# A two-layer graph network kernel: the first layer's row terms are spread by two DMAs instead of TensorE transposes, and the stages around them are reordered

## The chip, the cores and the metric

The kernel runs on one core of a Trainium2 chip. The metric is device time in microseconds (us); lower is better. The core has five engines that matter here: PE (TensorE, matrix products; PEld is its weight load), DVE (VectorE), ACT (ScalarE), POOL (GpSimd) and SP (SyncE, which here only issues DMAs). Each engine runs its own instructions strictly in their written order and waits where one of them needs a result that isn't there yet.

## The reference

Input `x` is 64 batches of 256 rows of 256 values; `adj` is one 256 x 256 adjacency mask for all batches. Two layers follow, each an attention over the graph and then a feed-forward part:

```python
x = x + _L0_gnn_ref(_layernorm(x), adj, L0_gnn_W, L0_gnn_a)   # 4 heads of 64
x = x + _L0_ffn_ref(_layernorm(x), L0_ffn_weight, L0_ffn_bias) # dense 256 -> 256
x = x + _L1_gnn_ref(_layernorm(x), adj, L1_gnn_W, L1_gnn_a)   # 1 head of 256
x = x + _L1_ffn_ref(_layernorm(x), L1_ffn_...)                 # 8 experts, top 2
```

In the first attention, `q = h @ W` is split into 4 heads; each row i has a term `e_src[i]` and each row j a term `e_dst[j]` per head; the score is `leaky_relu(e_src[i] + e_dst[j], 0.2)`, masked by `adj`, softmaxed over j, and multiplied with `q`. An elu follows.

## The kernel before

Everything is float32. A batch lies as 128 partitions x 2 halves (`NT` = 2) of rows. The softmax is computed without a sum in the exponent: since exp(max(a, b)) = max(exp a, exp b), the kernel takes exponentials of the row terms alone and forms each score as max(column value of i, scalar of j) times the mask. The scalar of j is a per-partition operand; the value of i has to stand in every partition along the free axis. That second form is the "row terms" of the change.

**What one batch does**, in `batch_layers`, a generator in which each `yield` ends a stage. `turned` (L114) turns blocks of x on DVE; `norm_stats` (L362) gives the norm's mean and variance on DVE and ends with two small POOL operations (L382, L383); `projected` (L429) multiplies with the weights on PE (L436) and takes three exponentials per head on ACT (L444); `scaled` (L449, L452) scales the values on DVE. `scores` (L500) then does, for two heads at a time, four PE transposes of one broadcast column each (L506), which put the row term of every i into all partitions of a PSUM bank, and four DVE operations (L513) that form the scores `z`. `attended` (L519) multiplies `z` with `q` on PE (L527) and inverts the sums (L534). DVE scales by them (L570), or ACT in the first 16 batches (`EARLY`, L565); ACT takes an exponential (L576) and DVE ends the elu and adds x (L579, L580, L583). The feed-forward part is a transpose on PE with a copy on ACT (`transposed`, L420, L426), a product (L591) and a DVE sum (L598) that gives `x2`. `norm_squares` (L392) squares on ACT (L401) and ends with two POOL operations (L411, L414). The second attention is `projected1` (L471, L478 to L484), `scores1` (L490, L495), `attended` and a relu on ACT (L614), with a DVE sum (L620) and squares again. Then `by` (L628, L631), the normalised rows and the base of the output on ACT (L640, L645), the store of the base by SP (L656), and the router's product (L670).

**The experts.** `route` decides for each chunk of batches which rows go where; POOL sends the rows to DRAM by indirect DMAs (L970). `expert_pair` loads 256 rows of one expert (SP, L804, L815) and its weights (L830), turns them on DVE (L116), multiplies twice on PE (L862 with Gelu on ACT L868; L877), DVE adds the bias (L887), ACT scales (L855), and POOL adds the rows into the output by indirect DMAs (L898). Two pairs run per batch once rows are there.

**What sets the order.** It is written out by a loop over steps, three to a batch (`TICKS`, phases 0, 1 and 2). In each step every active batch and job advances by one stage, in the order of the rank it yielded: a small rank is early in the step. A negative rank continues within the same step. So a batch's stages are spread over some 19 steps, and stages of about seven batches alternate in one period of three steps. A new batch begins in phase 2 at rank 25. All engines see their instructions in this order.

**Buffers.** `z` (6 buffers of 2 KB per partition), `xin` (6, loaded 3 batches ahead), the 8 PSUM banks that all products share. DMAs of SP and ACT share eight semaphores in turn; each waits for the one that last used its semaphore.

Of the kernel before, what the change touches and what calls it, by code (L numbers as in the profile page):

```python
# [9 lines left out]
F32 = mybir.dt.float32  # L10
I32 = mybir.dt.int32
AF = mybir.ActivationFunctionType
# [3 lines left out]
P = 128  # L16
# [11 lines left out]
def kernel(  # L28
# [17 lines left out]
    nc = tc.nc  # L46
# [47 lines left out]
    def load_batch(b):  # L94
        t = io.tile([P, NT, D], F32, tag="xin", name=f"xin_{b}", bufs=6)
        nc.sync.dma_start(
            out=t, in_=x_rows[b * N : (b + 1) * N, :].rearrange("(t p) d -> p t d", p=P)
        )
        return t
# [10 lines left out]
        return t  # L110

    S = 32

    def turned(dst, blocks):  # L114

# [371 lines left out]
    def scores1(ex, me):  # L487
        pd = bank("pd", [N])
        for t in range(NT):
            nc.tensor.transpose(  # L490
                pd[:, t * P : (t + 1) * P], ex[:, t, 1:2].to_broadcast([P, P]), ident
            )
        z = work.tile([P, NT, N], F32, tag="z", name="z", bufs=6)
        for j in range(NT):
            nc.vector.scalar_tensor_tensor(  # L495
                z[:, j, :], pd, ex[:, j, 2:3], me[:, j, :], op0=ALU.max, op1=ALU.mult
            )
        return z

    def scores(q, heads, hs, mask, probs):  # L500

        d = D // heads
        pd = bank("pd", [len(hs), N])
        for i, h in enumerate(hs):
            for t in range(NT):
                nc.tensor.transpose(  # L506
                    pd[:, i, t * P : (t + 1) * P],
                    q[:, t, h, d + 1 : d + 2].to_broadcast([P, P]), ident,
                )
        for i, h in enumerate(hs):  # L510
            z = work.tile([P, NT, N], F32, tag="z", name="z", bufs=6)
            for j in range(NT):
                nc.vector.scalar_tensor_tensor(  # L513
                    z[:, j, :], pd[:, i, :], q[:, j, h, d + 2 : d + 3], mask[:, j, :],
                    op0=ALU.max, op1=ALU.mult,
                )
            probs.append(z)

    def attended(q, heads, probs):  # L519

        d = D // heads
        pvs = []
        for t in range(NT):
            pv = bank("pv", [heads, d + 1])
            for h, z in enumerate(probs):
                for j in range(NT):
                    nc.tensor.matmul(  # L527
                        pv[:, h, :], z[:, j, t * P : (t + 1) * P], q[:, j, h, : d + 1],
                        start=(j == 0), stop=(j == NT - 1),
                    )  # L530
            pvs.append(pv)
        rinv = small.tile([P, NT, heads], F32, tag=f"rinv{heads}", name="rinv")
        for t, pv in enumerate(pvs):
            nc.vector.reciprocal(rinv[:, t, :, None], pv[:, :, d : d + 1])  # L534
        return pvs, rinv

    def batch_layers(b, c0, xng, lg):

        xb = xblk.pop(b)
        if b + BLOCKS_AHEAD < B:  # L540
            xblk[b + BLOCKS_AHEAD] = load_blocks(b + BLOCKS_AHEAD)
        xT = turned(work.tile([P, KT, N], F32, tag="xT", name="xT", bufs=4), xb)
# [12 lines left out]
        yield 10  # L555
        scores(q, H, range(2, 4), masks[0], probs)
        yield 50
        pvs, rinv = attended(q, H, probs)
# [38 lines left out]
        for t in range(NT):  # L597
            nc.vector.scalar_tensor_tensor(  # L598
                x2[:, t, :], pf[:, t, :], rstd[:, t : t + 1], x1b[:, t, :],
                op0=ALU.mult, op1=ALU.add, accum_out=sums[:, t : t + 1],  # L600
            )
# [8 lines left out]
        pvs, rinv = attended(q[:, :, None, :], 1, [z])  # L610
# [351 lines left out]
    def begin(job, rank):  # L962
        active.append([rank, len(order), job])
        order.append(job)
# [255 lines left out]
```

## Time and profile before

| | us |
|---|---|
| runs | 1582.44, 1584.82, 1584.85 (median 1584.82) |
| the profiled execution's own time | 1584.91 |
| its span, first to last instruction | 1583.0 |

All times of single operations below come from that one execution. The page's slices show how the busy share (in tenths) and the granted PE clock run over the 40 equal slices of the span:

```profile
PE   6999898899999999999999999999899998879996
DVE  6777777888888878888887878888788879555543
ACT  2676666576776777777777677667568898654332
PEclk9999999999999999999999999999999999889999
DMA  5721323456566657566666656675666766687853
```

Three stages can be told apart. Up to some 300 us few or no expert pairs are there; then the work of a batch and of two pairs repeats with a period of 21.33 us; after some 1300 us the batches are through the first layer and the remaining pairs and the dense last batches are worked off. The groups of the first layer's attention, costliest first (line, engine, operation, output<-input, shapes, count, then busy us, mean ns of one, idle time before and who ended it):

```profile
L527 PE MATMUL pv<-q,z 128*128 128x65 f32 (+1 forms) x2560 | 372.7, 300 | 5.9 <-issue 4.5
...
L436 PE MATMUL pq<-wx,xT 128*128 128x268 f32 x512 | 134.7, 408 | 3.2 <-DVE xT L116 2.6
```

The busy time of a PE group counts what isn't overlapped by the matmul before, so it is less than count times mean.

### The profile page before, as it was taken

Reading aid. Unit: us, or ns where it says so; the run is one execution under the profiler, and the core shown is the slowest. Engines: PE = TensorE matmul, PEld = TensorE weight load, DVE = VectorE, ACT = ScalarE, POOL = GpSimd, SP = SyncE. Lnnn points to the kernel's source line nnn. Section 1 sums busy time; section 2 is a strip of 40 time slices with the busy share of each in tenths; the row PEclk is TensorE's granted clock in tenths of the full one; section 3 lists DMA queues with packets and bytes.
Section 4 is the critical chain, followed back from the end, with each engine's and each line's share of the span. In section 5 each row is a group of like instructions: output and inputs, shape, how many; then the busy total and the mean of one; then the engine's idle time right before and its main releaser. Section 6 shows DMA issues by size and latency. Waiting matters only on the chain. (4 is left out here: it accounts for less than half of the span.)

```text
span 1583.0 us, 30896 instructions
## 1 busy us (share of the span) xinstructions
PE 1492.3 (94%) x8570; PEld 1316.6 (83%) x8570; DVE 1205.1 (76%) x4281; ACT 1044.4 (66%) x2515; POOL 862.5 (54%) x867
## 2 busy tenths in 40 slices
PE   6999898899999999999999999999899998879996
PEld 5888787788888888888888888888789887658885
DVE  6777777888888878888887878888788879555543
ACT  2676666576776777777777677667568898654332
POOL 2222536255756656565747575665665676743444
PEclk9999999999999999999999999999999999889999
DMA  5721323456566657566666656675666766687853
GB/s 147 217 55 48 94 69 88 114 125 138 140 137 149 146 115 156 128 153 131 159 132 130 140 141 137 149 147 110 155 135 147 145 139 120 140 193 169 158 100 50
DMA packets 361514, 207.61 MB, mean 131 GB/s; under 512 B 261496, under 2 KB 331648, under 8 KB 361344
## 3 DMA queue, kind: packets, MB, share of 16 engines
q1 hardware_dynamic: 311488, 138.31, 35.8%
q0 software_dynamic: 48864, 66.33, 23.0%
q8 instruction: 71, 1.16, 0.3%
q10 hardware_dynamic: 992, 0.99, 0.2%
q14 instruction: 99, 0.81, 0.2%
HBM read 117.43 MB, written 88.09 MB: 130 GB/s over the span
## 5 line engine op out<-in xcount | busy, mean ns | idle before, releaser
L898 POOL DMA_INDIRECT out_dram<-y,xt x258 | 412.0, 1597 | 176.8 <-issue 58.5
L527 PE MATMUL pv<-q,z 128*128 128x65 f32 (+1 forms) x2560 | 372.7, 300 | 5.9 <-issue 4.5
L527 PEld LDWEIGHTS pv<-q,z 128*128 128x128 f32 x2560 | 333.1, 194 | 19.6 <-issue 4.7
L877 PE MATMUL py<-w2s,hT 128*128 (+1 forms) x1224 | 284.8, 384 | 5.8 <-ACT hT L868 5.2
L970 POOL DMA_INDIRECT xs<-xng,pos x244 | 254.5, 1043 | 65.4 <-issue 60.7
L877 PEld LDWEIGHTS py<-w2s,hT 128*128 128x128 f32 x1224 | 230.4, 192 | 39.0 <-ACT hT L868 8.3
L862 PE MATMUL ph<-sT,we 128*128 128x256 f32 x1032 | 238.7, 381 | 3.3 <-DVE ohs L1099 2.9
L426 ACT COPY xT<-pt 128x512 f32<-128x512 f32 x192 | 113.3, 590 | 191.2 <-PE pt L420 142.5
L862 PEld LDWEIGHTS ph<-sT,we 128*128 128x128 f32 x1032 | 192.3, 191 | 28.4 <-DVE ohs L1099 3.3
L513 DVE SCALAR_TENSOR_TENSOR z<-pd,q,mask 128x256 f32<-128x256 f32 x512 | 211.2, 476 | 0.8 <-PE pd L506 0.8
L855 ACT ACTIVATE y<-y,w 128x256 f32<-128x256 f32 x258 | 112.5, 501 | 96.6 <-DVE y L887 87.6
L868 ACT ACTIVATE hT<-ph,we 128x256 f32<-128x256 f32 x306 | 123.4, 472 | 62.7 <-PE ph L862 40.9
L401 ACT ACTIVATE off<-x,sums 128x256 f32<-128x256 f32 x256 | 131.1, 512 | 40.3 <-DVE x L598 17.9
L471 PE MATMUL pq<-wx,xT 128*128 128x259 f32 x512 | 129.3, 394 | 19.3 <-ACT xT L426 11.7
L411 POOL TENSOR_SCALAR rstd<-sq 128x4 f32<-128x4 f32 (+1 forms) x66 | 12.8, 193 | 246.4 <-ACT off L401 246.1
L887 DVE TENSOR_TENSOR y<-py,b2s 128x512 f32<-128x512 f32 x129 | 86.9, 688 | 68.4 <-PE py L877 50.2
L436 PE MATMUL pq<-wx,xT 128*128 128x268 f32 x512 | 134.7, 408 | 3.2 <-DVE xT L116 2.6
L471 PEld LDWEIGHTS pq<-wx,xT 128*128 128x128 f32 x512 | 92.1, 190 | 45.8 <-ACT xT L426 19.9
L591 PE MATMUL pf<-wfT,xT 128*128 128x256 f32 x512 | 124.0, 386 | 0.1
L382 POOL TENSOR_SCALAR rstd<-mv 128x4 f32<-128x4 f32 (+1 forms) x66 | 15.4, 233 | 197.7 <-DVE mv L375 163.3
L436 PEld LDWEIGHTS pq<-wx,xT 128*128 128x128 f32 x512 | 99.4, 198 | 22.6 <-DVE xT L116 1.9
L591 PEld LDWEIGHTS pf<-wfT,xT 128*128 128x128 f32 x512 | 94.6, 195 | 10.9 <-DVE y L887 0.3
(165 smaller groups left out, 2552.5 us busy)
## 6 DMA issues: line engine op xcount, KB each, us to landing
we<-wpack SPq DMA_DIRECT2D x145, 288.0 KB
xr<-xs SPq DMA_DIRECT2D x516, 64.0 KB
xblk<-in_x_dram SPq DMA_DIRECT2D x256, 64.0 KB
xin<-in_x_dram SPq DMA_DIRECT2D x64, 256.0 KB
out_dram<-base SPq DMA_DIRECT2D x61, 256.0 KB
out_dram<-y,xt POOLq DMA_INDIRECT x258
xs<-xng,pos POOLq DMA_INDIRECT x244
xs<-fill SPq DMA_DIRECT2D x9, 260.0 KB
```

Of the source, the lines that this page charges most:

```text
L401: nc.scalar.activation(off, src[:, t, :], AF.Square, bias=sums[:, t : t + 1], scale=-float(D), accum_out=sq[:, at + t : at + t + 1],)
L426: nc.scalar.copy(dst, pt)
L436: nc.tensor.matmul(pq.rearrange("p h c -> p (h c)"), xT[:, k, t * P : (t + 1) * P], wx[:, k, :], start=(k == 0), stop=(k == KT - 1),)
L471: nc.tensor.matmul(pq, xT[:, k, t * P : (t + 1) * P], wx1[:, k, :], start=(k == 0), stop=(k == KT - 1),)
L513: nc.vector.scalar_tensor_tensor(z[:, j, :], pd[:, i, :], q[:, j, h, d + 2 : d + 3], mask[:, j, :], op0=ALU.max, op1=ALU.mult,)
L527: nc.tensor.matmul(pv[:, h, :], z[:, j, t * P : (t + 1) * P], q[:, j, h, : d + 1], start=(j == 0), stop=(j == NT - 1),)
L591: nc.tensor.matmul(pf[:, t, :], xT[:, k, t * P : (t + 1) * P], wfT[:, k, :], start=(k == 0), stop=(k == KT - 1),)
L862: nc.tensor.matmul(ph[:, f, :], we[:, k * D + f * P : k * D + (f + 1) * P], xT[:, k, :], start=(k == 0), stop=(k == KT - 1),)
L868: nc.scalar.activation(hT[:, f, :], ph[:, f, :], AF.Gelu, bias=we[:, C_B1 + f : C_B1 + f + 1])
L877: nc.tensor.matmul(py[:, t, :], hT[:, f, t * P : (t + 1) * P], w2s[:, e, f * D : (f + 1) * D].rearrange("p e c -> p (e c)"), start=(f == 0 ...
L898: d = nc.gpsimd.indirect_dma_start(out=out_rows, out_offset=bass.IndirectOffsetOnAxis(ap=xt[:, t, 0:1].bitcast(I32), axis=0), in_=y[:, t, ...
L970: d = nc.gpsimd.indirect_dma_start(out=xs_d[: E * CAP * PAIR, :], out_offset=bass.IndirectOffsetOnAxis(ap=at, axis=0), in_=xe, in_offset=None,
```

## The change

Four things change in `batch_layers` and its helpers.

1. **Row terms.** `scores` no longer transposes on PE. After `scaled`, `send_terms` turns the columns around the exponentials of `q` in 32 x 32 blocks on DVE into a small tile `ut`, so that a row term of 32 rows lies in one partition. An ACT-issued DMA writes 32 such runs (4 KB) to a DRAM tile of this batch. In the next step `spread_terms` issues, also from ACT, a DMA that reads the 4 KB into all 128 partitions, straight into the second half of the score tile `z4` (two buffers of 8 KB per partition). The score operations on DVE read it there, the last of them in place. `scores1` has its own tile `z1`.
2. **Stages of the first layer.** A batch (but the first) begins in phase 0, at rank 40, with the norm of x alone and then passes one step; the turn of x stays where it was. The projection moves from phase 1 to phase 0 (rank 60, its scaling and the first DMA at 65); the spreading takes phase 1 (rank 54); the scores stay in phases 2 and 0. The number of steps from the turn of x on is the same.
3. **The second layer's order.** Both `norm_squares` move to the start of the following step (ranks 7 and 6). The transposes of `x2` follow the first squares in the same step at rank 36, and so stand ahead of the second attention's product (rank 40). `by` is at rank 45, and the normalised rows and the base follow in the same step at rank 50.
4. **Early batches.** L565 on ACT is gone: DVE scales in every batch.

```diff
+    G = P // S
...
-        z = work.tile([P, NT, N], F32, tag="z", name="z", bufs=6)
+        z = work.tile([P, NT, N], F32, tag="z1", name="z1", bufs=1)
...
+    def send_terms(q, b):
+        ut = small.tile([P, S], F32, tag="ut", name="ut", bufs=1)
+        nc.vector.transpose(
+            ut.rearrange("p (t h w) -> p t h w", t=NT, h=H), q[:, :, :, HD - 1 : HD + 3]
+        )
+        ud = tc.dram_tile([S, S], F32, name=f"terms_{b}")
+        ud = ud.rearrange("c r -> (c r)").rearrange("(c p) -> c p", p=P)
+        return ut, ud
+
+    def spread_terms(ud):
+        z = work.tile([P, NT, NT, H, P], F32, tag="z4", name="z4", bufs=2)
+        nc.scalar.dma_start(
+            out=z[:, NT - 1].rearrange("p t h i -> p (t h i)"),
+            in_=rows_to_all(ud, S * S),
+        )
         return z
 
-    def scores(q, heads, hs, mask, probs):
-        d = D // heads
-        pd = bank("pd", [len(hs), N])
-        for i, h in enumerate(hs):
-            for t in range(NT):
-                nc.tensor.transpose(
-                    pd[:, i, t * P : (t + 1) * P],
-                    q[:, t, h, d + 1 : d + 2].to_broadcast([P, P]), ident,
-                )
-        for i, h in enumerate(hs):
-            z = work.tile([P, NT, N], F32, tag="z", name="z", bufs=6)
+    def scores(q, z, hs):
+        for h in hs:
             for j in range(NT):
                 nc.vector.scalar_tensor_tensor(
-                    z[:, j, :], pd[:, i, :], q[:, j, h, d + 2 : d + 3], mask[:, j, :],
+                    z[:, j, :, h, :], z[:, NT - 1, :, h, :], q[:, j, h, HD + 2 : HD + 3],
+                    masks[0][:, j, :].rearrange("p (t i) -> p t i", t=NT),
                     op0=ALU.max, op1=ALU.mult,
                 )
...
+        def first_norm():
+            x0 = xin.pop(b)
+            if b + AHEAD < B:
+                xin[b + AHEAD] = load_batch(b + AHEAD)
+            return x0, norm_stats(x0)[1]
+
+        if b:
+            x0, rstd = first_norm()
+            yield 99
+            yield 25
         xb = xblk.pop(b)
...
         xT = turned(work.tile([P, KT, N], F32, tag="xT", name="xT", bufs=4), xb)
-        yield 40
-        x0 = xin.pop(b)
-        if b + AHEAD < B:
-            xin[b + AHEAD] = load_batch(b + AHEAD)
-        _, rstd = norm_stats(x0)
-        yield 20
+        if not b:
+            x0, rstd = first_norm()
+        yield 60
         q, pqs = projected(xT, wx0, H, rstd)
-        yield -28
+        yield -65
         scaled(q, pqs, H, rstd)
+        ut, ud = send_terms(q, b)
+        nc.scalar.dma_start(
+            out=ud.rearrange("c (g r) -> g c r", g=G),
+            in_=ut[2 : P : S // (NT * H), :],
+        )
+        yield 54
+        z = spread_terms(ud)
         yield 10
-        probs = []
-        scores(q, H, range(0, 2), masks[0], probs)
+        scores(q, z, range(0, 2))
         yield 10
-        scores(q, H, range(2, 4), masks[0], probs)
+        scores(q, z, range(2, 4))
         yield 50
...
-            if early:
-                for h in range(H):
-                    nc.scalar.activation(
-                        hp[:, t, h * HD : (h + 1) * HD], pv[:, h, :HD], AF.Copy,
-                        scale=rinv[:, t, h : h + 1],
-                    )
-                continue
...
+        yield 7
         rstd = norm_squares(x2, sums)
-        yield 60
+        yield -36
         xT = transposed(x2)
...
+        yield 6
         rstd = norm_squares(x2, sums)
-        yield 80
+        yield 45
...
         nc.vector.tensor_scalar(by[:, 1], rstd, 1.0, None, op0=ALU.add)
-        yield 50
+        yield -50
...
-            if phase == 2 and more:
+            if more and (phase == 0 or step == 2):
...
-                    begin(nxt, 25)
+                    begin(nxt, 40 if phase == 0 else 25)
```

More of the change, by code (lines that the diff above doesn't have):

```diff
@@ L497, in scores1, with attended @@
             )
-        return z
-    def scores(q, heads, hs, mask, probs):
-        d = D // heads
-        pd = bank("pd", [len(hs), N])
-        for i, h in enumerate(hs):
-            for t in range(NT):
-                nc.tensor.transpose(
-                    pd[:, i, t * P : (t + 1) * P],
-                    q[:, t, h, d + 1 : d + 2].to_broadcast([P, P]), ident,
-                )
-        for i, h in enumerate(hs):
-            z = work.tile([P, NT, N], F32, tag="z", name="z", bufs=6)
+        return [z[:, j, :] for j in range(NT)]
+    def send_terms(q, b):
[12 more added lines that the diff above has]
+        )
+        return z
+    def scores(q, z, hs):
+        for h in hs:
             for j in range(NT):
                 nc.vector.scalar_tensor_tensor(
-                    z[:, j, :], pd[:, i, :], q[:, j, h, d + 2 : d + 3], mask[:, j, :],
+                    z[:, j, :, h, :], z[:, NT - 1, :, h, :], q[:, j, h, HD + 2 : HD + 3],
+                    masks[0][:, j, :].rearrange("p (t i) -> p t i", t=NT),
                     op0=ALU.max, op1=ALU.mult,
                 )
-            probs.append(z)
-    def attended(q, heads, probs):
+    def attended(q, heads, z):
         d = D // heads
@@ L524, in attended @@
             pv = bank("pv", [heads, d + 1])
-            for h, z in enumerate(probs):
+            for h in range(heads):
                 for j in range(NT):
                     nc.tensor.matmul(
-                        pv[:, h, :], z[:, j, t * P : (t + 1) * P], q[:, j, h, : d + 1],
+                        pv[:, h, :], z(j, h, t), q[:, j, h, : d + 1],
                         start=(j == 0), stop=(j == NT - 1),
@@ L542, in batch_layers @@
         xT = turned(work.tile([P, KT, N], F32, tag="xT", name="xT", bufs=4), xb)
-        yield 40
-        x0 = xin.pop(b)
-        if b + AHEAD < B:
-            xin[b + AHEAD] = load_batch(b + AHEAD)
-        _, rstd = norm_stats(x0)
-        yield 20
+        if not b:
+            x0, rstd = first_norm()
+        yield 60
         q, pqs = projected(xT, wx0, H, rstd)
-        yield -28
+        yield -65
         scaled(q, pqs, H, rstd)
+        ut, ud = send_terms(q, b)
[5 more added lines that the diff above has]
+        z = spread_terms(ud)
         yield 10
-        probs = []
-        scores(q, H, range(0, 2), masks[0], probs)
+        scores(q, z, range(0, 2))
         yield 10
-        scores(q, H, range(2, 4), masks[0], probs)
+        scores(q, z, range(2, 4))
         yield 50
-        pvs, rinv = attended(q, H, probs)
+        pvs, rinv = attended(q, H, lambda j, h, t: z[:, j, t, h, :])
         hp = work.tile([P, NT, D], F32, tag="hp", name="hp", bufs=1)
@@ L609, in batch_layers @@
         yield 40
-        pvs, rinv = attended(q[:, :, None, :], 1, [z])
+        pvs, rinv = attended(
+            q[:, :, None, :], 1, lambda j, h, t: z[j][:, t * P : (t + 1) * P]
+        )
         yield 5
```

## The prediction

> **What bounds the kernel now.** I read the page's busy shares first, then busy time by stage, then who waits for whom, then single periods of the timeline. The first part of the page names the busiest engine:
>
> ```profile
> PE 1492.3 (94%) x8570; PEld 1316.6 (83%) x8570; DVE 1205.1 (76%) x4281; ACT 1044.4 (66%) x2515; POOL 862.5 (54%) x867
> ```
>
> The share is an average, so the span is cut into three stages (columns: stage, its length, then busy us and instruction count of PE, PEld, DVE, ACT, POOL, then granted clock, DMA share, GB/s):
>
> ```profile
> 40.00:300.00 260.00, 234.63 (x1441) 205.04 (x1440) 198.62 (x699) 167.34 (x504) 94.17 (x124) 0.96 0.35 96
> 300.00:1300.00 1000.00, 982.64 (x5853) 878.92 (x5852) 821.48 (x2924) 726.88 (x1684) 612.99 (x602) 1.00 0.64 139
> 1300.00:1583.00 283.00, 247.40 (x1138) 209.61 (x1136) 159.82 (x580) 141.00 (x301) 144.99 (x114) 0.95 0.67 134
> ```
>
> In the middle 1000 us PE is busy for 98%; its waits there are small (PE alone, 300 to 1100 us):
>
> ```profile
> PE pq L471 <- issue: 6.2, 26, 0.2
> PE pq L471 <- ACT xT L426: 3.5, 11, 1.1
> ```
>
> One batch takes 21.33 us there (L490 starts at 323.61 and 344.94), and DVE and ACT have 18% and 27% of slack. So PE's work sets the middle stage. In the first stage PE idles 25.4 us of 260, 9.5 us of them before L670, whose xT copy comes late on ACT. The last stage has almost none of the changed work.
>
> **What the change removes.** The 512 transposes of L506:
>
> ```profile
> L506 PE MATMUL pd<-ident,q 128*128 128x128 f32 x512 | 77.7, 276 | 0.1
> L506 PEld LDWEIGHTS pd<-ident,q 128*128 128x128 f32 x512 | 62.0, 139 | 7.1 <-ACT q L444 0.8
> L513 DVE SCALAR_TENSOR_TENSOR z<-pd,q,mask 128x256 f32<-128x256 f32 x512 | 211.2, 476 | 0.8 <-PE pd L506 0.8
> ```
>
> PE gives up 77.7 us by its busy time, 62.0 by weight loads alone; by starts in one period (801.50 to 801.94 and 808.46 to 809.30) 1.28 us, of which 0.24 is a wait for ACT's xT. I take 77.7: 54.4 of it falls in the middle stage (the same windows for L506 alone), 19.7 in the first. ACT gives up 128 small copies of L565 in the first 16 batches (28.1 us); DVE does them instead, 32 x 408 ns (L570) = 13 us.
>
> **What it adds to DVE.** One 128x32 block transpose per batch. A 128x512 one takes 697 ns, and the least DVE row is 160 ns: between 0.1 and 0.3 us, I take 0.17; 11 us in all. The 512 score operations now read SBUF instead of PSUM. The same operation stands in the trace with both sources:
>
> ```profile
> L930 DVE SCALAR_TENSOR_TENSOR dbase<-py,wd,dbase x48: 476/480/485, 1425.8 to 1574.1; 128x256 f32<-128x256 f32 x48
> L930 DVE SCALAR_TENSOR_TENSOR dbase<-b2s,wd,dbase x48: 483/485/486, 1426.4 to 1574.6; 128x256 f32<-128x256 f32 x48
> ```
>
> 480 ns from PSUM, 485 from SBUF: no difference, and I count none. [...]
>
> **What it adds to ACT and the DMAs.** Two DMAs per batch on ACT's queue: 4 KB out, then 512 KB back. ACT's DMA issues at the start take 0.45 us each. Both are issued next to waits ACT has anyway (for DVE's y, then for PE's pt of L420), so their issue is covered. The bytes: queue q1 moved 138.31 MB in 35.8% of 16 engines' span, so 33.6 MB more are 8.7%, upon 64%. No row comes near saturation: from 1400 to 1500 us the share was 0.83 and PE still 93% busy.
>
> **One period walked through.** The rows I use (DVE, ACT, PE in turn):
>
> ```profile
> 801.71 0.48 DVE L598 SCALAR_TENSOR_TENSOR x<-pf,rstd,x1b 128x256 f32<-128x256 f32 x1 [0.72 <-PE pf L591]
> 802.93 0.51 ACT L401 ACTIVATE off<-x,sums 128x256 f32<-128x256 f32 x1
> 804.07 1.28 ACT L868 ACT_TABLE_LOAD   x1
> 805.36 1.57 ACT L868 ACTIVATE hT<-ph,we 128x256 f32<-128x256 f32 x4
> 808.66 0.58 ACT L426 COPY xT<-pt 128x512 f32<-128x512 f32 x1 [1.74 <-PE pt L420]
> 810.52 1.28 ACT L478 ACT_TABLE_LOAD   x1 [0.53 <-PE pq L471]
> 815.09 1.10 ACT L645 ACTIVATE base<-x,by 128x256 f32<-128x256 f32 x2
> ```
>
> Let 0 be the start of L478's table load (810.52), 1.22 after PE began L471. PE, with start-to-start times of this period in the new order: L471 -1.22, pt 0.64, L436 1.07, py 2.87, L490 6.33, pv 6.55, pt(xng) 10.07, pf 10.59, ph 12.32, pl 15.78, pt(x2) 16.59, second pv 17.02, L471 again 18.84. That is a period of 20.06. Do the others keep up? ACT ends base at 815.09 + 1.10 - 810.52 = 5.67, and both q exponentials (0.43 as a pair) at 6.1. DVE is ready at about 4.0 and waits for them. Then, by the durations of the same rows in this period: scaled 0.87, to 6.8; the block transpose, 7.0; two y of 0.69, 8.4; two sT, 1.30, 9.7; z 0.84, 10.5; rinv and hp 1.1, 11.6; the sum of x2 0.76, 12.4. The L598 operations wait for pf, which is read 1.94 us after its start, 12.53, and end at 13.4. ACT's four squares, 0.64 apart, begin with the first sum at 12.05 and end at 14.6; table load 15.9, Gelu 17.5, xT copy 18.05, while L471 needs it at 18.84. DVE goes on with x1 and x1b to 15.5, scores 17.1, the block turn 17.8, waits for the second pv to 19.2, then w, scores, norms and by (4.9), 24.1, which is 4.0 of the next period. So this circle ACT, DVE, ACT has 0.8 us left, where before it had about 1.9 (21.33 less 19.4: y was in ACT's part, but two y, two sT and z were not in DVE's). It holds, narrowly. A full chunk of four puts 1.2 us of routing (815.86 to 817.09) between y and sT: 0.5 us lost, 12 times, 6 us; bounds 0 and 16 (every one of the 20 chunks at 0.8).
>
> **The two new waits on ACT and DVE.** ACT's second DMA waits until the first has landed. Behind it queue the xT copy for L670, the exponential and the squares above. The first is issued at 7.0; with two issues (0.9) and the 7.2 us of ACT work from there to the end of the xT copy for L471 (0.58, 0.61, 2.56, 1.28, 1.57, 0.58) it may take 18.84 - 7.0 - 8.1 = 3.7 us to land before L471 is late. Nearest rows: SP's wait for a 1 KB load, and a row-add landing in DRAM in the last chain:
>
> ```profile
> SPq L293 <- DMA wt<-in_L_ffn_b_dram: 9.0, 4, 3.2
> 1561.48 4.15 DMA out_dram<-y,xt
> SPq L656 <- ACT base L645: 498.5, 53, 15.9
> ```
>
> So 2.1 (L284 issued at 31.86, L293 freed by 33.96) to 4.15; I take 2.5, nearest to a small plain transfer: hidden. At 4.15 it costs 0.5 us x 47 periods = 23 us. [...]
>
> The 512 KB are issued near 9.6 and DVE reaches the scores at 15.5: 5.9 us of room, and DVE stands 1.9 us before scaled anyway. ACT's broadcast load at the very start landed 4.4 us after its issue, adj_i 5.6: hidden, with little over.
>
> The third row of the last fence covers SP: DMAs of SP and ACT share semaphores in turn, so the second pair's xr loads now wait for the two transfers, some 5 us. SP idles 9.4 us per batch before the base store; without that cover sT would wait. The x norm moves a period ahead with its four DVE operations, its POOL pair and its xin load; xin has six buffers for 5.7 periods of life. The later squares put POOL's pair behind the sends and one row-add of that step; rstd is then ready at 15.9 and needed at 21.3, three row-adds of 1.6 us away. These go at nothing.
>
> At the start nothing hides the round trips: 2.1 + 4.4 us less a transpose, +5.5 (0 to 13, if two batches pay).
>
> **Sum.** 1583.0 - 77.7 + 6 + 5.5 = 1516.8 us of span. The profiled execution's own time is 1.9 above its span and 0.1 above the median, so 1518.6.
> Bounds: the first stage may also lose the 9.5 us before L670 and some 10 us of half clock (260 x 0.04): 1583 - 77.7 - 19.5 + 0 + 1.8 = 1488. With 62.0 instead of 77.7, +16 and +13: 1552.
>
> **Rivals.**
> The circle takes over: ACT's part is longer by 1.5 us than walked (a copy behind late work), so a period is 20.8: 47 x 0.75 = +35, 1554. For it: only 0.8 us left, DVE at 17.2 + 0.2 of 20.06. Against: each piece was read with its waits in.
> Slower: the 4 KB landing holds ACT. From 4.9 us on (3.7 + 1.28) the period is longer than 21.33. At 6 us it is 22.4: 47 x 1.07 and about 1 us for each of 16 early batches, +66, near 1650. For it: the row-adds need 3.7 to 4.15 us in a quiet tail. Against: each of those adds 128 KB to rows in DRAM, this one writes 4 KB.
> It does not do what it says: the transposes lay in cover (0.24 us of each period did, before L471) and PE waits elsewhere, 1585. Against: PE waits 9.7 us in 800.
>
> **How the numbers follow.** Forecast 0.70, circle 0.12, slower 0.14, nothing 0.04. About 0.2% (3 us) is what a measurement tells from no change: faster 0.82, same 0.04, slower 0.14. The range 1488 to 1560 holds the forecast and the circle.
>
> **What would show it.** L506 gone; two L490 about 20.1 us apart near 800 us; PE at 97% or more there. Wrong if ACT waits long before the spread (its xT copy of L426 late for L670), if DVE's first score operation waits for a DMA, or if PE waits for xT before L471 by over 0.5 us per period. The first stage should be some 20 us shorter.

## The result and the profile after

| kernel | runs, us | ratio to before, 95% interval | span, us | mean granted PE clock |
|---|---|---|---|---|
| before | 1584.84 (1582.44 to 1587.11) | 1 | 1583.0 | 0.981 |
| after | 1707.05 (1700.13 to 1711.5) | 1.0767 (1.0728 to 1.0807) | 1698.0 | 0.942 |

The change makes the kernel 122 us slower, where 66 us faster was forecast. First the busy shares, and the busy digits of PE with its granted clock over the 40 slices, from the page of the kernel after:

```profile
PE 1495.9 (88%) x8058; PEld 1301.3 (77%) x8058; DVE 1248.7 (74%) x4377; ACT 1022.7 (60%) x2387; POOL 888.2 (52%) x869
...
PE   4888888789898989899898989898899989868997
...
PEclk8998989989999999999999999999999999999999
```

The 512 transposes are gone (8570 instructions less 512 is 8058), yet PE's busy time has not fallen: 1495.9 against 1492.3. Without the 77.7 us of L506 it should be 1414.6, so the same products take 81 us more. And PE idles 202.1 us of the span instead of 90.7, 111 more. The two make 192.7 us, which is the whole distance from the sum's 1505.3 (1583.0 less 77.7) to 1698.0. By stage (the same windows and columns as before the change):

```profile
40.00:300.00 260.00, 218.21 (x1239) 187.83 (x1239) 199.36 (x696) 130.47 (x355) 92.17 (x116) 0.91 0.41 121
300.00:1300.00 1000.00, 909.00 (x5046) 797.97 (x5045) 776.84 (x2704) 652.17 (x1535) 573.20 (x552) 0.95 0.64 149
```

PE was busy 98% of the middle stage at a clock of 1.00; now 91% at 0.95. No other engine is near its limit. So nothing became a new bound; PE is made to wait. For whom, between 300 and 1100 us (waits: us in total, times, longest):

```profile
PE pq L472 <- ACT xT L427: 28.2, 15, 1.9
PE ph L884 <- DMA we<-wpack: 21.0, 5, 4.6
PE ph L884 <- DVE x1b L601: 7.6, 2, 4.4
```

```profile
DVE q L453 <- ACT q L445: 75.9, 34, 2.5
```

Two stories stand here: a copy on ACT that is late, with DVE waiting 2.2 us in nearly every period for ACT's q exponentials; and a weight load that comes late by DMA. One of the prediction's own signs of being wrong is here too: PE's wait for xT before this product, which it set at over 0.5 us per period, is 28.2 us in some 34 periods, 0.8 each.

**First story, the timeline of one period after** (start, duration, engine, line):

```profile
796.38 0.13 DVE L650 SCALAR_TENSOR_TENSOR by<-sums,rstd 128x2 f32<-128x2 f32 x1
...
796.55 1.09 ACT L662 ACTIVATE xng<-x,by,rstd 128x256 f32<-128x256 f32 x2 [0.22 <-DVE by L650]
...
797.54 1.07 ACT L667 ACTIVATE base<-x,by 128x256 f32<-128x256 f32 x2
...
798.53 0.41 ACT L445 ACTIVATE q<-pq,rstd 128x12 f32<-128x12 f32 x2
...
798.81 0.88 DVE L453 SCALAR_TENSOR_TENSOR q<-pq,rstd,q 128x256 f32<-128x256 f32 x2 [2.22 <-ACT q L445]
```

DVE ends `by`; ACT was waiting for just that, makes `xng` and `base` (2.1 us), and only then the q exponentials (their product, L437, ended at 797.16), for which DVE has been standing since `by`. `scaled` is at the head of DVE's work of the next period, and `by` is at its end: a circle DVE, ACT, DVE, whose length is all of DVE's work in a period plus this stand.

**Second story, the DMA queues in the same stretch** (SPq and ACTq are the issuing queues):

```profile
799.97 0.52 ACTq L572 DMA_DIRECT2D terms<-ut  x1
...
801.92 0.33 ACTq L515 DMA_DIRECT2D z<-terms  x1
...
802.03 0.98 SPq L852 DMA_DIRECT2D we<-wpack  x2
...
803.61 0.41 SPq L678 DMA_DIRECT2D out_dram<-base  x1
...
809.64 1.93 SPq L826 DMA_DIRECT2D xr<-xs  x4
...
809.93 6.66 PE L884 MATMUL ph<-sT,we 128*128 128x256 f32 x16 [3.34 <-DMA we<-wpack]
```

The 4 KB write lands in 1.95 us (issue to the issue of the DMA that waits for it). At that moment SP, too, can go on: its `we` pair had stood for the same landing (in the trace the write and the first load of the pair use the same one of the eight semaphores). The store of `base`, ready at 798.6, goes at 803.61 behind it, and the next xr loads stand 5.5 us for the spread. PE then waits 3.34 us for `we`, whose data are there only 7.9 us after the pair's issue: the pair moves beside the 512 KB issued just ahead of it, at a DMA share of 0.94 (first window below). So both a late issue and a transfer of up to 7.9 us are in this wait. And its product takes 6.66 us instead of the 3.6 of other periods. The queue's own waits over the whole span show how often:

```profile
SPq L826 <- DMA z<-terms: 104.3, 32, 5.5
SPq L852 <- DMA terms<-ut: 100.3, 11, 11.8
...
SPq L826 <- DMA terms<-ut: 24.1, 10, 11.1
```

Why did the product take twice as long? Busy time and clock in four stretches around it:

```profile
806.00:809.90 3.90, 0.59 (x3) 0.19 (x1) 3.07 (x10) 2.75 (x10) 0.91 (x2) 0.90 0.94 304
809.90:813.40 3.50, 3.47 (x8) 2.86 (x9) 2.22 (x5) 1.25 (x1) 2.87 (x3) 0.50 0.75 184
813.40:816.70 3.30, 3.30 (x13) 2.67 (x11) 0.00 (x0) 0.91 (x3) 2.82 (x2) 0.61 0.49 101
816.70:825.00 8.30, 8.30 (x47) 7.33 (x47) 5.25 (x25) 6.00 (x13) 0.38 (x1) 1.00 0.76 177
```

After the idle time the granted clock is 0.50 for 3.5 us, and back at 1.00 only some 7 us later. So a wait of PE can be paid for again. By the mean clock (an estimate: span times one less the clock) 98 us of PE's work are lost to it after, and 30 before: most of the 81 us by which busy time is too long.

### The profile page after: what moved, and what is told of

Read it like the earlier page. It is cut to its first block, busy times and chain, and to the rows that moved or that the text cites. A ratio compares the mean times of both kernels' runs of the same rounds, so it can differ in the third digit from the quotient of the medians.

```text
span 1698.0 us, 29954 instructions
## 1 busy us (share of the span) xinstructions
PE 1495.9 (88%) x8058; PEld 1301.3 (77%) x8058; DVE 1248.7 (74%) x4377; ACT 1022.7 (60%) x2387; POOL 888.2 (52%) x869
## 5 line engine op out<-in xcount | busy, mean ns | idle before, releaser
L539 PEld LDWEIGHTS pv<-q,z 128*128 128x128 f32 x2560 | 338.0, 196 | 15.1
L884 PE MATMUL ph<-sT,we 128*128 128x256 f32 x1032 | 259.9, 405 | 49.0 <-DMA we<-wpack 23.8
L884 PEld LDWEIGHTS ph<-sT,we 128*128 128x128 f32 x1032 | 206.6, 204 | 89.6 <-issue 26.9
L525 DVE SCALAR_TENSOR_TENSOR z<-z,q,mask 128x256 f32<-128x256 f32 x512 | 242.1, 493 | 37.3 <-DMA z<-terms 27.9
L899 PEld LDWEIGHTS py<-w2s,hT 128*128 128x128 f32 x1224 | 234.3, 192 | 45.0 <-ACT hT L890 11.2
L472 PE MATMUL pq<-wx,xT 128*128 128x259 f32 x512 | 148.6, 440 | 55.7 <-ACT xT L427 49.4
L472 PEld LDWEIGHTS pq<-wx,xT 128*128 128x128 f32 x512 | 107.2, 215 | 87.8 <-ACT xT L427 61.5
L453 DVE SCALAR_TENSOR_TENSOR q<-pq,rstd,q 128x256 f32<-128x256 f32 x128 | 56.1, 479 | 140.3 <-ACT q L445 133.2
L437 PE MATMUL pq<-wx,xT 128*128 128x268 f32 x512 | 138.7, 418 | 17.6 <-DVE xT L117 11.9
L662 ACT ACTIVATE xng<-x,by,rstd 128x256 f32<-128x256 f32 x128 | 69.9, 594 | 124.8 <-DVE by L650 124.8
L437 PEld LDWEIGHTS pq<-wx,xT 128*128 128x128 f32 x512 | 101.4, 208 | 37.0 <-DVE xT L117 9.5
```

The costliest lines, as they stand in the source:

```text
L437: nc.tensor.matmul(pq.rearrange("p h c -> p (h c)"), xT[:, k, t * P : (t + 1) * P], wx[:, k, :], start=(k == 0), stop=(k == KT - 1),)
L472: nc.tensor.matmul(pq, xT[:, k, t * P : (t + 1) * P], wx1[:, k, :], start=(k == 0), stop=(k == KT - 1),)
L525: nc.vector.scalar_tensor_tensor(z[:, j, :, h, :], z[:, NT - 1, :, h, :], q[:, j, h, HD + 2 : HD + 3], masks[0][:, j, :].rearrange("p (t i ...
L539: nc.tensor.matmul(pv[:, h, :], z(j, h, t), q[:, j, h, : d + 1], start=(j == 0), stop=(j == NT - 1),)
L884: nc.tensor.matmul(ph[:, f, :], we[:, k * D + f * P : k * D + (f + 1) * P], xT[:, k, :], start=(k == 0), stop=(k == KT - 1),)
L899: nc.tensor.matmul(py[:, t, :], hT[:, f, t * P : (t + 1) * P], w2s[:, e, f * D : (f + 1) * D].rearrange("p e c -> p (e c)"), start=(f == 0 ...
```

## The experiments

The theory: two causes, the circle and the DMAs on ACT's queue, which add up. Rivals: it is one cause (one hides or makes the other); the round trip over DRAM costs by its landing or its bytes, whoever issues it; part 3 of the change (the second layer's order) is the harm. In the runs called "without DMAs", and in e13 and e16, the row terms are not spread: the score operations read a row of the mask in their place, with the same shapes. All times are medians, with the ratio to before and its 95% interval. Beside the different groups of runs, before itself had medians from 1580.25 to 1586.83 us, so a difference between times of two groups is good to some 7 us.

### Undoing one part (e1, e2), part 3 alone (e3, e9)

e1 puts the order of part 3 back in the kernel after (the transposes of x2 stay at rank 36); e2 leaves both DMAs out of it; e3 is the kernel before with only the diff of part 3; e9 the kernel before with one line of it.

```diff
e1, in the kernel after:                e3, in the kernel before:
-        yield 7                        +        yield 7
         rstd = norm_squares(x2, sums)           rstd = norm_squares(x2, sums)
-        yield -36                      -        yield 60
+        yield 36                       +        yield -36
...
-        yield 6 ... yield 45           -        yield 80
+        yield 80                       +        yield 6 ... yield 45
...
-        yield -50                      -        yield 50
+        yield 50                       +        yield -50
e9, in the kernel before:  -  yield 60  +  yield 36   (transposes of x2)
```

> The changed kernel with both norm_squares back in the step of their sums (ranks 70 and 60), by a step ahead of the normalised rows again, the turn of x2 still ahead of the second attention's product. Circle theory (DVE's by, ACT's rows and base, ACT's q exponentials, DVE's scaled stand in one step, so DVE waits 2.2 us in every period): DVE no longer holds ACT's rows, the 125 us of ACT waiting for by go, about 1640 us. SP theory (the weights' load waits behind ACT's small DMA): the waits of L884 for we remain and little changes, 1690 us or more.

> The changed kernel without its two DMAs per batch: the row terms are left out, the scores read a mask in their place, so the output is another; order of all other work kept. SP theory: the stalls of PE before the experts' first product (3 to 4.6 us, about once in four batches, each with a half-clock window of 3.4 us) go, 11 x 6 us, about 1640 us, and more if the round trips cost in the first stage. Circle theory: the DVE wait of 2.2 us per batch stays and the time stays within 20 us of the changed kernel.

> The kernel before with only the second layer's order changed (later squares, turn of x2 ahead of the product, by and rows in one step). If later squares alone hold PE (the transposed x2 reaches L471 late): 1610 us or more. Circle theory: here y, sT and z stand between by and scaled, so DVE doesn't wait and the time is 1585 us within 15.

> The kernel before with the transposes of x2 one step part earlier (rank 36 instead of 60, ahead of the second attention's product), squares and all else as before. If the gain of the third part alone (1537 us) comes from that product covering ACT's copy of x2: about 1540 us. If it comes from the later squares: 1575 us or more.

| run | us | ratio |
|---|---|---|
| e1_squares_back | 1648.78 | 1.0392 (1.0335 to 1.045) |
| e2_no_dmas | 1593.32 | 1.0062 (1.003 to 1.0094) |
| e3_before_part3 | 1536.64 | 0.9686 (0.9631 to 0.9741) |
| e9_turn_only | 1564.88 | 0.9867 (0.9839 to 0.9896) |

The DMAs cost 114 us (1707 to 1593); that is all in which the two kernels differ, the score operations' source and the round trips at the start included. But without them the kernel is still no faster than before, although L506 is gone. e2 fits neither of its forecasts (about 1640, or within 20 us of 1707).

Part 3 by itself is no harm: on the kernel before it gains 48 us, where no gain was expected, and the one line of e9 gains 22 of them. Yet taking it out of the kernel after gains 58. So its harm comes from standing together with part 2: with it, `xng` and `base` (rank 50) are on ACT just ahead of the q exponentials (rank 60). In e1 DVE's wait for them falls to 13.3 us between 300 and 1100 us.

### The circle (e6, e7)

Both are without DMAs. e6 also has e1's edit. e7 leaves part 3 in and moves the projection, so that ACT makes the q exponentials ahead of `xng` and `base`:

```diff
-        yield 60
+        yield 33
         q, pqs = projected(xT, wx0, H, rstd)
-        yield -65
+        yield -47
         scaled(q, pqs, H, rstd)
```

> The changed kernel without its two DMAs (row terms left out, a mask read in their place) and with both squares back in the step of their sums. Circle theory: neither of the two costs is left, DVE waits little before scaled, the period falls to some 20.5 us and the time to 1535 us or less. If something third holds PE (the transposes of x2, the clock), it stays near the 1593 us of the kernel without DMAs.

> The changed kernel without its two DMAs (row terms left out, a mask read in their place), later squares kept, but the projection at rank 33 and its scaling at 47 in the same step, so that ACT takes the q exponentials ahead of the normalised rows and the base, and DVE's scaled follows by without a wait. Circle theory: DVE's 2.2 us before scaled go, 1593 us fall to about 1520. If DVE's wait before scaled costs nothing: within 15 us of 1593.

e6: 1567.1, 0.9881 (0.983 to 0.9932). e7: **1511.65, 0.9532 (0.9504 to 0.9559)**. Two ranks in two lines are worth 82 us (1593 to 1512).

e6 misses its forecast of 1535 or less. Undoing part 3 gains 26 us here, where it gained 58 with the DMAs (e1), so e1's gain was not the circle's alone. DVE's wait for q is down to 17.8 us in e6 and its middle periods to 20.4 us on average (by the starts of L491 from the 21st to the 53rd batch, here and below), but it also gives up what part 3 gains, and it is 31 us behind e7 by the 16th batch; why was not followed.

DVE's idle time before `scaled` between 300 and 1100 us, first in e2, then in e7:

```profile
DVE q L453 <- ACT q L445: 86.2, 38, 3.0
```

```profile
DVE q L453 <- issue: 1.4, 1, 1.4
```

From the page of e7, and its windows:

```profile
PE 1425.8 (94%) x8058; PEld 1259.3 (83%) x8058; DVE 1239.8 (82%) x4377; ACT 1019.1 (67%) x2387; POOL 889.7 (59%) x869
```

```profile
300.00:1300.00 1000.00, 976.90 (x5706) 874.69 (x5706) 871.07 (x3166) 772.66 (x1764) 675.31 (x640) 1.00 0.67 146
```

PE is at 98% and the clock at 1.00 again, with L506's work gone: the span is 73.0 us under before's, where the sum had 77.7 less 11.5 of losses. But e7 holds part 3 too, which gained 48 by itself, so the 73 are not L506's alone. The circle is thereby shown: only an order was changed, and PE's own order in the period (L472, L421, L437, L902) is the same in the timelines of e2 and e7 near 800 us, so it is not a better cover on PE that made the gain. (In e17 below, with the DMAs on SP and the projection late, the wait is back at 82.2 us in the same window; in e11, early with the DMAs on ACT, it is 6.8 over the whole span.)

### Who issues the DMAs (e4, e8, e11, e12, e17)

```diff
e4: the we pair loaded a stage earlier, behind the xr loads   (kernel after)
-        yield 90
         we = io.tile([P, WROW], F32, tag="we", name="we", bufs=WBUFS)
         nc.sync.dma_start(out=we, ...)
+        yield 90
e8, e17, e12: both DMAs of the row terms
-        nc.scalar.dma_start(
+        nc.gpsimd.dma_start(      e8,  kernel after
+        nc.sync.dma_start(        e17, kernel after; e12, with e7's projection
e11: the kernel after with e7's projection, DMAs on ACT
```

> The changed kernel with the experts' weights loaded one step earlier, together with their rows. SP theory: the waits of L884 for we go, 11 x 6 us, about 1640 us. Circle theory: no change beyond 20 us.

> The changed kernel with both DMAs issued by POOL instead of ACT, which have other semaphores than SP's and don't stand in ACT's queue. SP theory: SP no longer waits for either, PE's waits for we go, 1630 us or less. Rival, that the transfers themselves (512 KB a batch on the DMA engines) or their landing cost the time: 1680 us or more.

> The changed kernel with its two DMAs, and the projection 27 ranks earlier, so that the q exponentials stand ahead of xng and base on ScalarE (the edit that brought the kernel without the DMAs from 1593 to 1512). Theory (two causes that add up: the circle by-xng-base-q, and the DMAs on ScalarE's queue that SyncE's loads wait for): the circle's share goes and the DMAs' price stays, 1707 less about 82 is 1625, 1590 to 1640. Rival (one cause: the DMAs cost only because the circle makes them late): they are hidden once it is gone, 1512 to 1535. A third way: they overlap, so that the earlier sends change little, above 1660.

> As the run before, but both DMAs issued by SyncE, in its own order with its loads: no load then waits for a transfer that another engine has not issued yet. Theory (the price of the DMAs is that SyncE's loads wait by a semaphore for a small DMA that stands later in ScalarE's order, and then TensorE stands for the we pair): most of the price goes, 1515 to 1560. Rival (the landing and the spread cost what they do, whoever issues them, because VectorE's scores wait for them): as the run with ScalarE's issue, within 15 us. Second rival (SyncE itself now stands until VectorE's turn and until the landing, and its loads come late): slower than with ScalarE's issue.

> The changed kernel with one edit: both DMAs issued by SyncE instead of ScalarE; the projection stays late. Theory (two causes that add up): the circle's 80 stay on the 1543 of the early projection, 1610 to 1635. Rival (with the circle there is no room for SyncE's stand either): 1660 and above. If the circle mattered only with ScalarE's DMAs: about 1545 to 1590.

| DMAs of the row terms | projection as in the change | projection early (e7's) |
|---|---|---|
| none | e2: 1593.32 | e7: 1511.65 |
| issued by ACT | after: 1707.05 | e11: 1616.65, 1.0225 (1.0207 to 1.0242) |
| issued by SP | e17: 1633.1, 1.0329 (1.0288 to 1.0371) | e12: 1543.14, 0.9778 (0.9751 to 0.9806) |
| issued by POOL | e8: 1821.08, 1.1483 (1.1449 to 1.1516) | |

e4: 1660.98, 1.0469 (1.0392 to 1.0547). The two causes nearly add: the early projection gains 82, 90 and 90 us in the three rows, and the DMAs on ACT cost 114 and 105 us in the two columns. Moving them to SP gives 74 us back in both (by the ratios 69 and 71). With SP issuing, the same 33.6 MB move and DVE waits for them as before, so neither the bytes nor the landing made those 74. In e12's middle stage (windows; then two of the queue's own waits over the whole span, for DVE's turn and for the landing):

```profile
300.00:1300.00 1000.00, 974.87 (x5697) 873.97 (x5696) 885.92 (x3146) 767.57 (x1755) 664.47 (x629) 0.99 0.75 170
```

```profile
SPq L572 <- DVE ut L505: 278.1, 50, 11.9
...
SPq L515 <- DMA terms<-ut: 72.6, 55, 3.6
```

PE is at 97% with the DMA share at 0.75. SP now stands itself, 50 times for DVE's turn and 55 times for a landing (1.3 us each), longer in all than it stood for ACT's DMAs; yet PE's waits for `we` are gone from the list of waits between 300 and 1100 us, in e12 and in e17: the loads behind are early enough. What hurt was not that SP waits but for what, as these waits read: in e12 SP's loads stand 8.2 us in its list for the spread (L826 3.3, L106 3.0, L852 1.9) and in no row of it for the write; in the kernel after, L826 stood 104.3 us for the spread and L852 100.3 for the write, each a DMA that stands later in time on another engine's queue, behind that engine's waits.

e4, 46 us faster than after and short of its forecast of 1640, shows that no single load is at fault: with `we` out of the way SP's waits went to the xt and x loads (L837 81.2 us, L106 80.6), and PE still waits 12.3 us for `we` in the 800 us. e8 misses its forecast of 1630 or less although what that was built on came true: no wait for the terms is left in SP's list. On POOL the DMAs stand behind its own row-adds, and the spread is late: DVE waits 90.8 us for z between 300 and 1100 us, where it waited 5.3.

### Write alone, spread alone, ACT's stand alone (e13, e14, e16)

All have the early projection. e13 keeps the 4 KB write on ACT and no spread; e14 keeps the spread on ACT, always of batch 0's terms, so that 63 writes go; e16 has no DMA, but ACT copies `ut` where the write stood.

```diff
e13:  -  z = spread_terms(ud)              e14:  +  if b == 0: (write)
      +  z = work.tile([...], bufs=2)            +  ud = first_terms[0]
e16:  +  nc.scalar.copy(us, ut)            (no DMA)
```

> Early projection, the 4 KB write kept on ScalarE's queue, the 512 KB spread left out (the scores read a mask in place of the row terms). Theory (SyncE's loads wait for the small DMA): a good part of the price stays, 1540 to 1600, and SyncE's waits for a transfer of the terms stay in the list of waits. Rival (the spread's transfer or its wait on ScalarE is the price): 1510 to 1525, as without DMAs.

> Early projection, the 512 KB spread kept for every batch but always from batch 0's terms in DRAM, so that 63 of the 64 small writes go and no spread waits for a landing (other batches' row terms are those of batch 0). Theory (SyncE's loads wait for the small DMA): 1512 to 1535, the spread is hidden. Rival (the 33 MB of the spread or their wait in VectorE's scores are the price): as with both DMAs, 1590 or more.

> Early projection, no DMA for the row terms (the scores read a mask in their place), but at the write's place ScalarE copies the turned terms, so that it stands there until VectorE has turned them, as the write did. Theory (the 25 us that the write alone cost come by SyncE's loads): 1510 to 1518, as without it. Rival (ScalarE's own stand holds xng, base and the xT copies back): 1530 to 1540.

e13: 1536.48, 0.9723 (0.9707 to 0.9739). e14: 1569.16, 0.9929 (0.9906 to 0.9951). e16: 1520.07, 0.9602 (0.9586 to 0.9618). Against e7's 1512 the write costs 25 us and the spread 57; both together cost 105 (e11), 23 more than the sum. The 23 were not taken apart; ACT's stand for the landing, for one, is in none of the three. By the starts of L491, 17 of the write's 25 are lost by the 16th batch already, and 10 of the spread's 57. ACT's stand for DVE's turn (e16) explains some 8 to 11 of the write's 25 (by the times, by the ratios), so a part of them is ACT's own. In e14 the score operations write over their source, in e7 and e13 they don't; by e18 below that is some 8 to 12 of the 57. Each of the three results lies between its two forecasts, and for the DMAs the theory had named the wrong DMA: it had made the small write the culprit and the spread free. First a stretch of e14's timeline, then a row of its queue's waits:

```profile
803.62 0.33 ACTq L515 DMA_DIRECT2D z<-terms  x1
...
808.29 0.98 SPq L857 DMA_DIRECT2D we<-wpack  x2
```

```profile
SPq L857 <- DMA z<-terms: 114.8, 10, 12.6
```

The `we` pair waits till the spread has landed, 4.7 us after its issue; every fourth period is then 22.6 to 26.8 us long and the others 19.9 to 20.5. So either DMA on ACT's queue holds SP's loads (L852's 100.3 us for the write in the kernel after, L857's 114.8 for the spread here), and the larger one costs more by itself, 57 us to 25.

### What is left with SP issuing (e15, e18, e19)

e12 is 31 us over e7. By the starts of L491, it is 21 us behind at the 21st batch and 30 at the 63rd, with nearly equal periods in the middle (20.15 us on average, e7's 20.11). e15 gives batch 0 alone its row terms by the old PE transposes; e18 puts the row terms in a tile of their own (two buffers; the score tile then has one); e19 uses PE transposes and ACT's scaling (old L565) for the first 16 batches and DRAM for the other 48.

```diff
e15:  +  turn = b < 1         e19:  +  turn = b < EARLY   (and L565 back)
      +  if turn: nc.tensor.transpose(pd[...], q[...].to_broadcast([P, P]), ident)
e18:  -  z[:, j, :, h, :], z[:, NT - 1, :, h, :], q[...]
      +  z[:, j, :, h, :], rows[:, :, h, :], q[...]
```

> Early projection, both DMAs issued by SyncE, and batch 0 alone gets its row terms by transposes on TensorE as before the change, so that nothing waits for a round trip over DRAM at the start. Theory (the 31 us over the kernel without DMAs are mostly the start): 1520 to 1532. Rival (they are the transfers' load on the whole first stage, or on every period): 1538 to 1545.

> Early projection, both DMAs issued by SyncE, the row terms in a tile of their own, so that no score operation writes the tile that it reads. Theory (the slower score operations come from reading the tile they write): a group of four takes about 1.67 us again, and the time is 8 to 15 us under the 1543 of the same kernel with one tile, 1528 to 1535. Rival (they are slower for another reason, such as the transfers' traffic): 1.9 us per four, 1540 to 1546.

> Early projection, SyncE issues both DMAs, but the first 16 batches get their row terms by transposes on TensorE and their hp by ScalarE, as before the change; only batches 16 to 63 go over DRAM. Theory (what is left over the kernel without DMAs lies in the first 16 batches, where VectorE waits 16.8 us for landings and pays 8 us for slower score operations and 13 us for hp, while TensorE has about 30 us of idle time for 19.7 us of transposes): 1500 to 1520, faster than every kernel so far. Rival (TensorE becomes the bound there and gives it back): 1535 to 1550.

| run | us | ratio |
|---|---|---|
| e15_sp_first_turned | 1542.76 | 0.973 (0.9705 to 0.9754) |
| e18_sp_rows_apart | 1534.81 | 0.9702 (0.9672 to 0.9731) |
| e19_sp_early_turned | **1512.28** | 0.956 (0.953 to 0.9589) |

The start is not it: e15 gains 3 us by the second batch and has lost them again by the 16th. e18 gains 8 us by the times, 12 by the ratios. Score operations after (two, then four of them), and the four in e18:

```profile
809.66 1.00 DVE L525 SCALAR_TENSOR_TENSOR z<-z,q,mask 128x256 f32<-128x256 f32 x2
...
809.66 1.91 DVE L525 SCALAR_TENSOR_TENSOR z<-z,q,mask 128x256 f32<-128x256 f32 x4
```

```profile
811.74 1.66 DVE L526 SCALAR_TENSOR_TENSOR z<-rows,q,mask 128x256 f32<-128x256 f32 x4
```

Four took 1.65 from PSUM before. In e18 each ends 0.39 us after the one ahead of it; after the change, those that overwrite their own row terms take 0.52. So a group of four takes as long from SBUF as from PSUM, and writing over the source makes it longer. (The whole group of 512 falls from 244.4 us in e12 to 225.2 in e18, against 211.2 before; the rest of that difference was not followed.) And e19 takes away what the first 16 batches pay on DVE, which is nearly as busy there as PE: in e12 it works 220.23 of the 260 us between 40 and 300 us and waits 16.8 us for landings.

```profile
PE 1430.4 (95%) x8186; PEld 1268.5 (84%) x8186; DVE 1223.2 (81%) x4329; ACT 1048.5 (69%) x2515; POOL 889.9 (59%) x869
```

```profile
40.00:300.00 260.00, 249.20 (x1603) 221.54 (x1603) 217.12 (x795) 187.22 (x558) 108.87 (x140) 0.99 0.43 119
```

The page of e19 and its first stage: PE is busy 96% there where e12 had 229.57 us of 260. e19 beats both kernels, 0.956 of before, and it has its row terms, which e7 leaves out. How much of its 31 us is the landing, the source tile and the scaling was not taken apart.

## Why the prediction was wrong, step by step

- **L506, 77.7 us.** Not shown by itself. PE's group of 77.7 us is gone, but e7, 73.0 us under before in span, also holds part 3 with its 48. Beside e3, which has part 3 and L506, e7 is 25 us faster, and its middle periods are 20.1 us instead of 20.9: 0.8 us, where 77.7 us over 64 batches would be 1.2. That e7 and e19 end at 1512, near the forecast's 1518.6, is therefore luck as far as the sum goes: a gain that it put at nothing fills the gap.
- **"DVE is ready at about 4.0 and waits"; "0.8 us left … It holds, narrowly".** The step that failed. The walk had the two numbers: `by` at 4.0 of the next period, and ACT's `xng` of the period it began with, 814.10 less 810.52 = 3.58. `xng` needs `by`, so it can't start then. The stand before `scaled` (1.9 us) was read as slack of DVE; it is a link of the circle. Its length by the walk's own numbers is DVE's work from 5.9 to 24.1 (18.2, its waits in it) and, as the timeline after shows, 2.3 us from the end of `by` (796.51) to `scaled` (798.81): 20.5 us, 21.7 where routing adds its 1.2, against PE's 20.06. In e2 the middle periods are 19.9 to 24.6 us, 21.4 on average, and in e7 20.1. It cost 82 us (e2 to e7), four times what 47 periods of the difference of 0.44 make: 22 of the 82 are lost by the 16th batch, which the walk does not cover, and by the mean clock (0.970 and 0.982; an estimate, span times one less the clock) some 20 are PE's lower clock after its waits. The rival "the circle takes over" had the mechanism, without this link and at less than half its price.
- **The landing, 2.5 us, hidden up to 3.7.** Right in length: 1.95 us in the timeline above, 2.1 to 2.4 in its neighbours. It was hidden mostly, not wholly: ACT's xT copy waits for landings ten times in the run, 18.2 us in all. The rival "the 4 KB landing holds ACT" named the right place, and for the most part the wrong victim: ACT's stand for DVE's turn is worth some 8 to 11 us (e16); its stand for the landing was not run alone.
- **"DMAs of SP and ACT share semaphores in turn", SP's idle 9.4 us as cover, "These go at nothing".** The second step that failed, and the dearest: the DMAs cost 105 to 114 us, of which 74 go with the issuer. The coupling was seen, but only the xr loads were put behind it, and with a wait of one transfer. `we`, x and the base store queue behind it as well, and the wait begins from whenever ACT comes to issue: 11.8 us at the longest, more than the 9.4.
- **Score operations "none".** The two rows (480 and 485 ns) were right about the source's place. But the new form writes over its source: 242.1 us instead of 211.2. It is hidden in the middle stage (20.15 us a period in e12, 20.09 in e18) and costs some 8 to 12 us by e18.
- **The start, +5.5 (0 to 13).** Too small, and in the wrong place: with SP issuing, 22 us are lost against e7 by the 16th batch (e12), and not by the first round trip (e15) but over 16 batches in which DVE has little slack; e19 gets 31 back there.
- **Later squares, at nothing.** Part 3 was left out of the sum: by itself it gains 48 us (e3), a gain that the circle ate in the kernel after.
- **The clock** stood in the bounds as 10 us of half clock. Many waits of PE drew a second loss after them (last section); the mean clock fell from 0.981 to 0.942.
- **Block transposes** took 0.21 us, 0.17 had been taken. Part 4's 13 us on DVE went at nothing; they lie in the stage where DVE has little slack. Neither was run alone.

## What to carry to other kernels

When a walk through one period ends with an engine that waits, follow the wait round: if what it waits for waits in turn for the end of that engine's own work a period earlier, the wait is no slack but a part of the period. And price an order in pairs: a move that gains alone (here 48 us for part 3) can, together with another, put two instructions next to each other on one engine that must not be.

In this kernel a DMA that waits for fresh data belonged on the queue whose other DMAs come after it anyhow. On a queue that shared semaphores with another engine's loads it made these loads wait for it (moving both DMAs to SP gave 74 us back), and the cost showed as idle time of engines that never touch its data; look for it in the issuing queue's own waits.

## What the runs showed of the hardware

**Half clock after short idle times.** In e2, PE stands 1.89 us before L472, and its eight products take 3.22 us where they take 1.91 in the next period. Windows around that point:

```profile
803.90:807.30 3.40, 3.40 (x23) 2.84 (x21) 3.25 (x8) 3.27 (x9) 1.28 (x2) 1.00 0.45 89
807.30:809.20 1.90, 0.06 (x1) 0.00 (x0) 1.87 (x9) 1.90 (x6) 1.70 (x2) 1.00 0.58 149
809.20:812.60 3.40, 3.35 (x10) 2.61 (x11) 3.26 (x12) 2.51 (x5) 1.92 (x2) 0.60 0.99 239
812.60:816.00 3.40, 3.40 (x17) 3.01 (x16) 1.42 (x8) 3.40 (x10) 1.64 (x4) 0.89 0.18 29
```

PE was busy throughout until 807.3; one idle time of 1.9 us was enough for a clock of 0.60 in the next 3.4 us. Not every such wait does it: of the ten of 1.88 or 1.89 us before L472 between 300 and 1110 us of e2, five are followed within 3.4 us by a stretch of half clock, and of the nine of 1.59 to 1.71 us none.

**Writing over the source.** A score operation that writes the 128x256 values it reads as its first operand ends 0.52 us after its predecessor (kernel after) instead of 0.39 (e18), an eighth of a microsecond each, for 256 of the 512 operations.

**POOL as issuer** made both DMAs dearer than either other engine, 1821 us: 114 more than with ACT, 188 more than with SP.
